# A third way of splitting the combined weights: 18 blocks of products in stage 3, R's sums bank by bank, S2's sum on VectorE, a scaled identity on ScalarE

## The chip, the cores and the metric

The kernel runs on one core of a Trainium2 chip. The metric is the device time of one execution in microseconds; the kernel before took 480.68 us (median of 3 runs, 479.33 to 481.21). A core has TensorE for matrix products (PE, its weight loads are listed as PEld), VectorE (DVE), ScalarE (ACT), GpSimd (POOL) and SyncE (SP), which here issues the transfers. SBUF is the on-chip memory, PSUM the banks that TensorE writes its products into.

## The reference

128 samples x of 64 channels and 1024 positions pass four convolutions of three taps, whose weights are scaled per sample by a style vector and normalised; the second doubles the length, the fourth halves it again. The input is added at the end.

```python
s = style @ mw.T + mb
weight = SCALE * w * s[:, None, :, None]
demod = lax.rsqrt(jnp.sum(weight * weight, axis=(2, 3)) + EPS)
weight = weight * demod[:, :, None, None]
# 'same':       conv of 3 taps, + b
# 'upsample':   transposed conv of stride 2, + b, then a blur of (1, 3, 3, 1) / 8 times 2
# 'downsample': a blur of (1, 3, 3, 1) / 8, then a conv of stride 2, + b
for i, typ in enumerate(('same', 'upsample', 'same', 'downsample')):
    out = _layer(out, style, weights[i], biases[i], mod_w[i], mod_b[i], typ)
return x + out
```

Nothing nonlinear stands between the layers, so for one sample they are one convolution of nine taps and stride one over x, with edge effects at the two ends.

## The kernel before

For each group of four samples (q, 32 of them) the kernel first multiplies the four layers' small weight matrices into one table of nine taps, and then runs this one convolution over the samples. All is in 32-bit floats. Four samples fill the 128 partitions twice (two of 64 channels in each), so a product stands as four matrix instructions, one for each quadrant of 64 x 64; the profile records each of them twice.

*The weights of a group* come in stages, each a set of small products in PSUM and copies that scale them per sample on ScalarE. `scale3` scales the last layer's weights (wd). `stage1_a` and `stage1_b` multiply them with the third layer's into S (five tap matrices; some are formed as sums and differences, which saves products). `share`, `share_copy` and `stage2_rest` multiply S with E, the second layer's taps with its blur, into R (seven matrices; two sums of pairs are kept beside them, formed by `r_sums` on GpSimd). `stage3_b` and `stage3_a` multiply R with the first layer's weights into the nine taps W. Products that are shared are made in `stage3_b`, in a bank of psA that is free just then; ScalarE copies them into psW, and `stage3_a` accumulates the rest on top.

*Combining.* The nine taps are used in groups of three positions (three kinds: a, b, c), and the convolution uses the Toom scheme: five products m0 to m4 with three taps each instead of nine. `combine_a` and `combine_b` on VectorE form the weights h1, h2, h3 from a, b, c; `residual` adds the identity matrix (the final "x +"), scaled per sample by a table t3, to the middle tap.

*The convolution.* `conv0` to `conv4` are these five products, 12 matrix instructions of 340 columns each. conv3, conv1, conv2 and conv0 accumulate one after the other in the same bank psA, and what stands there in between is picked up: `copy_m3` (ScalarE), `sum1` and `sum2` (VectorE). `sum2` runs after conv2: it writes 3 x m3 + psA into the bank Y, on which conv4 then accumulates, and subtracts psA from y1w. `outputs` scales the three result planes on ScalarE, and SyncE stores them.

*Order.* The program's order is written out by hand (`turn_of(q)` for q = 4 to 28, `early_turn` for the first four, a tail for the last three); each engine executes its own instructions strictly in that order and waits where data or a buffer is missing. A turn q works on four groups at a time: convolutions of q and n = q + 1, stage 2 and 3 of c = q + 2, stage 1 of s = q + 4. In a turn from q = 5 on TensorE runs: stage 2 of c, conv2 of q, `stage3_b` of c, conv4 of q, `stage3_a` of c, conv3 of n, `stage1_a` of s, conv0 of q, `stage1_b`, `share`, conv1 of n. psW, psS and psR share the same two PSUM banks (pool `ps_w`, one buffer), so each must be read out before the next is written. The lines of the profile are those of helpers: L753 is `product` (all five convolutions), L571 `same_row` (stage 3), L467 `chain_matmul` (stage 2), L389 `tap_matmul` (stage 1), L360 `scaled_copy` (ScalarE's scaled copies), L662 `sum_of` (VectorE), L588 `r_sums`, L445 and L442 the ends of `stage1_b`, L659 `residual`, L812 the subtraction in `sum2`, L726 and L731 `in1` and `in2` on GpSimd, L711 `in3` on VectorE.

## Time and profile before

| | |
|---|---|
| time of the kernel, median of 3 runs | 480.68 us (479.33, 480.68, 481.21) |
| profiled execution: span from first to last instruction | 478.0 us |
| granted clock of TensorE, mean | 0.997 |
| busy: TensorE, VectorE, ScalarE, GpSimd | 469.6, 417.5, 310.1, 163.5 us |
| convolutions of 340 columns (L753), three groups of it | 187.3, 63.9, 62.8 us |
| transfers | 70.70 MB, mean 148 GB/s |

Of the profiled execution the profile gives the span alone; the three times above are of executions without a profile, and the median lies 2.7 us above the span. In rows of groups the columns are the line, the engine, the operation, output and inputs, shapes and count, then busy time and mean duration of one in ns, and after the second bar the engine's idle time before them with what ended it. In rows of a timeline they are start and duration in us; several alike are merged, and in square brackets stands idle time ahead. Matrix instructions overlap, so that the start of the next is a better measure of a product's cost than its recorded duration.

### The profile page before, as it was taken

What the parts mean: (1) busy time and instruction counts of PE and PEld (TensorE: products, weight loads), DVE (VectorE), ACT (ScalarE), POOL (GpSimd) and SP (SyncE); (2) the same over time, 40 slices, a digit from 0 to 9 for tenths busy, and PEclk for the clock granted to TensorE, in tenths of its full rate; (3) what the DMA queues carried; (4) which work ended last, traced back from release to release, by engine and by line L of the source; (5) the groups of instructions that cost most, each with busy time, mean ns of one, the idle gap of its engine ahead of it and who ended that gap; (6) DMA issues with size and microseconds to landing.
All of it is one profiled execution on the core that took longest, in us unless ns stands there. A gap on an engine that the chain in (4) does not pass through costs nothing.

```text
span 478.0 us, 26721 instructions
## 1 busy us (share of the span) xinstructions
PE 469.6 (98%) x11928; PEld 346.4 (72%) x11928; DVE 417.5 (87%) x690; ACT 310.1 (65%) x708; POOL 163.5 (34%) x197
## 2 busy tenths in 40 slices
PE   8999999999999999999999999999999999999995
PEld 7877788777878876677776677766887777766652
DVE  5889998879889998899979899979989999999895
ACT  5565666667666676666667666667666768766352
POOL 3434032663335342243432233422434432333200
PEclk9999999999999999999999999999999999999998
DMA  5406365544445554345543455533455554445125
GB/s 175 158 28 200 114 195 192 150 139 144 139 150 157 173 173 127 122 151 160 171 149 120 131 170 152 173 127 126 145 169 162 162 154 146 152 146 170 61 91 191
DMA packets 50514, 70.70 MB, mean 148 GB/s; under 512 B 5664, under 2 KB 47328, under 8 KB 50400
## 3 DMA queue, kind: packets, MB, share of 16 engines
q1 hardware_dynamic: 49808, 68.32, 45.8%
q8 instruction: 93, 1.52, 1.5%
q10 hardware_dynamic: 592, 0.69, 0.5%
q14 instruction: 21, 0.17, 0.1%
HBM read 35.36 MB, written 33.62 MB: 144 GB/s over the span
## 4 chain that ended last, share of the span: by engine, by line
PE 95%; DVE 4%; issue 0%; ACT 0%; ACTq 0%; DVEq 0%
PE psA L753 45%; PE Y L753 11%; PE psR L467 9%; PE psA L571 7%; PE psW L571 7%; PE psS L389 6%; PE psR L533 4%; PE psA L467 2%; PE Y L994 2%; DVE H L662 1%; PE Y L180 1%; PE Y L336 1%; DVE G L662 0%; PE psM L204 0%; DVE o L832 0%
## 5 line engine op out<-in xcount | busy, mean ns | idle before, releaser
L753 PE MATMUL psA<-T,H 64*64 64x340 f32 x2304 | 187.3, 447 | 0.8 <-DVE y L662 0.7
L753 PEld LDWEIGHTS psA<-T,H 64*64 64x64 f32 x2304 | 89.9, 133 | 50.0 <-issue 3.1
L662 DVE SCALAR_TENSOR_TENSOR G<-X 128x1376 f32<-128x1376 f32 (+2 forms) x65 | 78.1, 1207 | 1.1 <-DMA X<-in_x 0.9
L726 POOL TENSOR_TENSOR T<-G 128x684 f32<-128x684 f32 x28 | 46.5, 1659 | 73.1 <-DVE G L662 73.1
L445 POOL TENSOR_TENSOR S<-S 128x128 f32<-128x128 f32 x28 | 22.1, 790 | 144.1 <-ACT S L360 136.8
L360 ACT ACTIVATE R<-psR,tC 128x448 f32<-128x448 f32 x63 | 36.5, 630 | 46.3 <-PE psR L467 26.7
L753 PE MATMUL psA<-T,Wf 64*64 64x340 f32 x768 | 63.9, 446 | 0.0
L753 PE MATMUL Y<-T,Wf 64*64 64x340 f32 x768 | 62.8, 451 | 0.1
L662 DVE SCALAR_TENSOR_TENSOR Y<-m,psA 128x340 f32<-128x340 f32 x64 | 33.1, 517 | 28.0 <-PE psA L753 26.6
L360 ACT ACTIVATE psW<-psA 128x128 f32<-128x128 f32 x100 | 19.3, 269 | 50.3 <-PE psA L571 46.2
L740 DVE TENSOR_TENSOR T<-G 128x1368 f32<-128x1368 f32 (+1 forms) x33 | 50.7, 1540 | 0.0
L360 ACT ACTIVATE Wf<-psW,t 128x256 f32<-128x256 f32 (+2 forms) x76 | 32.7, 479 | 26.5 <-PE psW L571 26.2
L711 DVE TENSOR_TENSOR T<-X 128x684 f32<-128x684 f32 x32 | 47.9, 1496 | 0.0
L467 PE MATMUL psR<-S,E 64*64 64x64 f32 (+1 forms) x1472 | 46.5, 238 | 0.0
L731 POOL TENSOR_TENSOR T<-G 128x684 f32<-128x684 f32 x28 | 46.5, 1660 | 0.0
L389 PEld LDWEIGHTS psS<-wd,w2n 64*64 64x64 f32 x1120 | 35.0, 133 | 13.3 <-ACT S L360 0.8
L467 PEld LDWEIGHTS psR<-S,E 64*64 64x64 f32 x1472 | 39.6, 134 | 5.2 <-ACT psR L490 0.2
L753 PEld LDWEIGHTS Y<-T,Wf 64*64 64x64 f32 x768 | 29.6, 132 | 18.0 <-DVE Y L662 0.7
L830 ACT ACTIVATE o<-psA,tb,td 128x340 f32<-128x340 f32 x63 | 37.0, 647 | 6.3 <-PE psA L753 6.3
L753 PEld LDWEIGHTS psA<-T,Wf 64*64 64x64 f32 x768 | 29.1, 133 | 15.1
L830 ACT ACTIVATE o<-Y,tb,td 128x340 f32<-128x340 f32 x63 | 36.6, 637 | 4.5 <-PE Y L753 2.7
L830 ACT ACTIVATE o<-y,tb,td 128x340 f32<-128x340 f32 x62 | 38.5, 679 | 0.6 <-DVE y L812 0.6
(165 smaller groups left out, 832.4 us busy)
## 6 DMA issues: line engine op xcount, KB each, us to landing
out<-o SPq DMA_DIRECT2D x167, 170.0 KB, 2.6
X<-in_x SPq DMA_DIRECT2D x150, 172.0 KB, 3.6
X<-in_x SPq DMA_DIRECT2D x14, 516.0 KB, 5.3
out<-o SPq DMA_DIRECT2D x6, 510.0 KB, 5.4
out<-o SPq DMA_DIRECT2D x2, 340.0 KB, 3.0
Xe<-in_x_ends SPq DMA_DIRECT2D x1, 512.0 KB, 6.7
out<-o ACTq DMA_DIRECT2D x3, 170.0 KB, 2.3
par<-in_params SPq DMA_DIRECT2D x2, 192.0 KB, 3.4
```

The costliest lines, as they stand in the source:

```text
L360: nc_a.activation(dst, src, AF.Copy, scale=f)
L389: nc.tensor.matmul(ps[r][cols, at * C : (at + n) * C], weight[rows], wd[c if r == 0 else 1 - c][rows, taps], start=first, stop=last, skip_ ...
L445: nc_g.tensor_add(t[:, :, 2], t[:, :, 2], t[:, :, 0])
L467: nc.tensor.matmul(dst[r][cols], weight[rows], st[c if r == 0 else 1 - c][rows, slots, :], start=False, stop=last, skip_group_check=True,)
L571: nc.tensor.matmul(dst[r][cols], weight[rows], t[rows, c, slots, :], start=first, stop=last, skip_group_check=True,)
L662: nc_v.scalar_tensor_tensor(out, x, f, y, op0=ALU.mult, op1=op)
L711: nc_v.tensor_sub(t[:, pairs, 0, :NJ], plane(X, 3, pairs), plane(X, 1, pairs))
L726: eng.tensor_add(t[:, :, 0, :NJ], plane(g, 2), plane(g, 1))
L731: eng.tensor_sub(t[:, :, 1, :NJ], plane(g, 2), plane(g, 1))
L740: nc_v.tensor_sub(t[:, pairs, :, :NJ], both(a, PL), both(b, 1))
L753: nc.tensor.matmul(ps[s][cols, :NB], w, Ts[q, tag][rows, c, i, g : g + NB], start=(g == 0 and m == 3), stop=(g == K - 1), skip_group_check ...
L830: nc_a.activation(dst, src, AF.Identity, bias=add, scale=d3)
```

## The change

Stage 3 is split anew. Before, two shared sums of pairs of R and 10 further blocks of 64 columns were made in `stage3_b`, 7 blocks in `stage3_a`. Now R has three sums of pairs (slots 7 to 9), one operation for each of its two banks; `stage3_b` multiplies them and makes 3 further blocks, and `stage3_a` makes 12 blocks: 18 in all for 19. ScalarE's copies into psW become two (each block written to two places) instead of four. The nine taps now lie in their natural order in W (`tap`, `TAPS`), and `stage3_a`'s result is scaled by kind with three tables t0, t0b, t0c, in six copies for two; `stage3_b`'s own result is two taps for five.

S is stored in another order (slots) and with other signs: even matrices at 2, 4, 6 and odd at 3, 5, with the sign in En (negated taps of E) instead of w2n and tBn. `stage1_b` forms on VectorE three matrices for two in one operation, and GpSimd's addition to S (L445) goes. `sum2` writes both banks of Y in one operation. `identity(n)`, two scaled copies on ScalarE after stage 2, makes x3, and `residual` adds it in one operation for two. In turns from q = 5 on the first third of conv0 of q moves ahead of `stage1_a`. The direct form of stage 1 (first groups) takes one product of three blocks for each tap.

```diff
...
@@ -293,12 +293,13 @@
     def table_B(bs):
         table(nc_g, tB, bs, ALT, DOWN, sc[:, 2, bs], sc[:, 1, bs])
 
-    def table_Bn(bs):
-        qs = slice(bs.start // 4, bs.stop // 4)
-        nc_g.tensor_scalar_mul(tBn[:, qs], tB[:, qs], -1.0)
-
     def table_0(bs):
         table(nc_g, t0, bs, ALT, ODD, sc[:, 0, bs], 1.0)
+
+
+    def table_0_kinds():
+        for t, f in ((t0b, 1.0 / 3.0), (t0c, -2.0)):
+            nc_g.tensor_scalar_mul(t, t0, f)
 
 
     def table_C(bs, eng=nc_g):
@@ -363,13 +364,17 @@
 
 
     w3x = const.tile([P, 5, C], F32, name="w3x")
-    w2n = const.tile([P, 5, C], F32, name="w2n")
+    w2n = const.tile([P, 2, C], F32, name="w2n")
+    En = const.tile([P, 4, C], F32, name="En")
 
     def split_weights():
         nc_g.tensor_copy(w3x[:, :K], w3)
-        nc_g.tensor_scalar_mul(w2n[:, :K], woi[2], -1.0)
-        for t, src in ((w3x, w3), (w2n, woi[2])):
-            nc_g.tensor_add(t[:, K:], src[:, : K - 1], src[:, 1:])
+        nc_g.tensor_add(w3x[:, K:], w3[:, : K - 1], w3[:, 1:])
+        nc_g.tensor_add(w2n, woi[2][:, : K - 1], woi[2][:, 1:])
+        nc_g.tensor_scalar_mul(w2n, w2n, -1.0)
+
+    def negated_taps():
+        nc_g.tensor_scalar_mul(En, E[:, 1:8:2], -1.0)
 
     DIRECT = 3
 
...
@@ -423,26 +429,26 @@
 
         ps = ps or unit(ps_w, f"psS{q}")
         wd = chain[q]
-        tap_matmul(ps, wd, 2, 2, w2n[:, 0, :], EVEN, first=True)
-        tap_matmul(ps, wd, 3, 2, w2n[:, 2, :], EVEN)
-        tap_matmul(ps, wd, 1, 1, w2n[:, 1, :], slice(1, 2))
+        tap_matmul(ps, wd, 3, 2, woi[2][:, 0, :], EVEN, first=True)
+        tap_matmul(ps, wd, 4, 2, woi[2][:, 2, :], EVEN)
+        tap_matmul(ps, wd, 2, 1, woi[2][:, 1, :], slice(1, 2))
         st, t = s_tiles(q)
         for r in range(2):
-            scaled_copy(nc_a, flat(st[r][:, :4]), ps[r][:, C : 5 * C], tBn[:, q, r : r + 1])
+            src = ps[r][:, 2 * C : 6 * C].rearrange("c (a o) -> c a o", o=C)
+            scaled_copy(nc_a, st[r][:, 0:7:2], src, tB[:, q, r : r + 1])
         chain[q] = wd, ps, st, t
 
     def stage1_b(q):
 
         wd, ps, st, t = chain[q]
-        tap_matmul(ps, wd, 2, 1, w2n[:, 3, :], slice(3, 4))
-        tap_matmul(ps, wd, 4, 1, w2n[:, 4, :], slice(4, 5), last=True)
+        tap_matmul(ps, wd, 3, 1, w2n[:, 0, :], slice(3, 4))
+        tap_matmul(ps, wd, 5, 1, w2n[:, 1, :], slice(4, 5), last=True)
         for r in range(2):
-            p1 = st[r][:, 0:1, :].to_broadcast([P, 2, C])
-            sums = ps[r][:, 2 * C : 6 * C].rearrange("c (a b o) -> c a b o", a=2, b=2)[:, :, 0]
+            p1 = st[r][:, 0:1, :].to_broadcast([P, K, C])
+            sums = ps[r][:, 3 * C : 6 * C].rearrange("c (a o) -> c a o", o=C)
             nc_v.scalar_tensor_tensor(
-                st[r][:, 4:6, :], sums, tB[:, q, r : r + 1], p1, op0=ALU.mult, op1=ALU.subtract
+                st[r][:, 3:6, :], sums, tB[:, q, r : r + 1], p1, op0=ALU.mult, op1=ALU.add
             )
-        nc_g.tensor_add(t[:, :, 2], t[:, :, 2], t[:, :, 0])
         chain[q] = st
         whole[q] = t
 
...
@@ -540,17 +547,17 @@
                     )
         if between:
             between()
-        t = r_pool.tile([P, 2, 9, C], F32, tag="R", name=f"R{q}")
+        t = r_pool.tile([P, 2, 10, C], F32, tag="R", name=f"R{q}")
         for r in range(2):
-            scaled_copy(engs[r], flat(t[:, r, :7]), ps[r][:, : 7 * C], tC[:, q, r : r + 1])
+            scaled_copy(engs[r], flat(t[:, r, :7]), ps[r][:, C : 8 * C], tC[:, q, r : r + 1])
         chain[q] = t
         return ps
 
 
-    TAPS = slice(3, 9, 2), slice(4, 9, 2), slice(0, 3)
+    TAPS = slice(0, 9, 3), slice(1, 9, 3), slice(2, 9, 3)
 
     def tap(kind, g):
-        return range(9)[TAPS[kind]][g]
+        return K * g + kind
 
     def new_w(q):
         Wq[q] = (
...
@@ -577,15 +584,20 @@
                     skip_group_check=True,
                 )
 
-    def stage3_out(q, ps, at, n, engs=(nc_a, nc_a)):
-        W = Wq[q][0]
+    def w_by_group(q, r):
+        return Wq[q][0][:, :, r].rearrange("c (g k) o -> c g k o", k=K)
+
+    def stage3_out(q, ps, kinds, engs=(nc_a, nc_a)):
         for r in range(2):
-            src = ps[r][:, : n * C].rearrange("c (a o) -> c a o", o=C)
-            scaled_copy(engs[r], W[:, at : at + n, r], src, t0[:, q, r : r + 1])
+            n = len(kinds)
+            src = ps[r][:, : n * K * C].rearrange("c (g k o) -> c g k o", k=n, o=C)
+            dst = w_by_group(q, r)[:, :, kinds[0] : kinds[0] + n]
+            scaled_copy(engs[r], dst, src, t0[:, q, r : r + 1])
 
     def r_sums(q, eng):
         t = chain[q]
-        eng.tensor_add(t[:, :, 7:9], t[:, :, 2:6:3], t[:, :, 3:7:3])
+        for r in range(2):
+            eng.tensor_add(t[:, r, 7:10], t[:, r, 0:6:2], t[:, r, 1:7:2])
 
     shared_w = {}
 
@@ -594,35 +606,36 @@
         new_w(q)
         t = chain[q]
         plan = (
-            (slice(0, 3), w0s[2][:, 2, :], slice(0, 7, 3)),
-            (slice(0, 2), w0s[2][:, 1, :], slice(1, 5, 3)),
-            (slice(0, 2), w0s[2][:, 0, :], slice(2, 6, 3)),
-            (slice(3, 4), w0s[0][:, 0, :], slice(0, 1)),
-            (slice(4, 5), w0s[1][:, 0, :], slice(1, 2)),
-            (slice(4, 5), w0s[1][:, 1, :], slice(0, 1)),
-            (slice(5, 7), w0s[0][:, 1, :], slice(7, 9)),
+            (slice(3, 4), w0s[1][:, 2, :], slice(5, 6)),
+            (slice(3, 4), w0s[1][:, 1, :], slice(6, 7)),
+            (slice(4, 5), w0s[2][:, 2, :], slice(6, 7)),
+            (slice(0, 3), woi[0][:, 1, :], slice(7, 10)),
         )
         for i, (at, weight, slots) in enumerate(plan):
             same_row(blocks(ps, at), weight, t, slots, i == 0, i == len(plan) - 1)
         pw = shared_w[q] = unit(ps_w, f"psW{q}")
-        src = blocks(ps, slice(5, 7))
-        for i, f in enumerate((1.0, 1.0 / 3.0)):
-            for dst, v in zip(blocks(pw, slice(i, i + 3, 2)), src):
-                scaled_copy(nc_a, dst, v, f)
-        stage3_out(q, ps, 0, 5)
+        for r in range(2):
+            src = ps[r][:, : K * C].rearrange("c (a o) -> c a o", o=C)
+            dst = pw[r][:, C : 7 * C].rearrange("c (a b o) -> c a b o", b=2, o=C)
+            nc_a.copy(dst, src[:, :, None, :].to_broadcast([P, K, 2, C]))
+        for r, src in enumerate(blocks(ps, slice(3, 5))):
+            scaled_copy(nc_a, Wq[q][0][:, 7:9, r], src, t0[:, q, r : r + 1])
 
     def stage3_a(q):
 
         t, pw = chain[q], shared_w.pop(q)
         plan = (
-            (slice(0, 3, 2), Wd[:, 0], slice(3, 7, 3)),
-            (slice(0, 3, 2), w0s[0][:, 2, :], slice(1, 5, 3)),
-            (slice(1, 4, 2), Wd[:, 1], slice(2, 6, 3)),
-            (slice(1, 2), w0s[1][:, 0, :], slice(4, 5)),
+            (slice(1, 6, 2), Wd[:, 0], slice(1, 6, 2)),
+            (slice(2, 7, 2), Wd[:, 1], slice(0, 5, 2)),
+            (slice(0, 7, 2), woi[0][:, 0, :], slice(0, 7, 2)),
+            (slice(3, 6, 2), woi[0][:, 2, :], slice(1, 4, 2)),
         )
         for i, (at, weight, slots) in enumerate(plan):
             same_row(blocks(pw, at), weight, t, slots, last=i == len(plan) - 1)
-        stage3_out(q, pw, 5, 4)
+        for kind, scale in enumerate((t0, t0b, t0c)):
+            at = slice(kind, 7, K)
+            for r, src in enumerate(blocks(pw, at)):
+                scaled_copy(nc_a, Wq[q][0][:, at, r], src, scale[:, q, r : r + 1])
 
     def stage3(q, part, pool=None, engs=(nc_a, nc_a)):
 
@@ -648,15 +661,17 @@
                     n == 1,
                     n == K * len(kinds),
                 )
-        stage3_out(q, ps, *((3, 6), (0, 3))[part], engs)
+        stage3_out(q, ps, kinds, engs)
         return ps
 
+    def identity(q):
+        for r in range(2):
+            nc_a.activation(x3[:, r], idn3, AF.Copy, scale=t3[:, q, r : r + 1])
+
     def residual(q):
 
-        W = Wq[q][0]
-        for r in range(2):
-            v = W[:, tap(1, 1), r, :]
-            nc_v.scalar_tensor_tensor(v, idn3, t3[:, q, r : r + 1], v, op0=ALU.mult, op1=ALU.add)
+        v = Wq[q][0][:, tap(1, 1)]
+        nc_v.tensor_add(v, v, x3)
 
     def sum_of(out, x, f, y, op=ALU.add):
         nc_v.scalar_tensor_tensor(out, x, f, y, op0=ALU.mult, op1=op)
@@ -806,8 +821,8 @@
     def sum2(q, steps=(0, 1)):
         if 0 in steps:
             m3 = m3c.pop(q)
-            for s, a in enumerate(banks(q)):
-                sum_of(Y[:, s, :NB], m3[:, s], 3.0, a[:, :NB])
+            for s, a in parts(q):
+                sum_of(Y[:, s, :NB], m3[:, s], 3.0, a)
         for s, a in parts(q) if 1 in steps else ():
             nc_v.tensor_sub(y1w[q][:, s], y1w[q][:, s], a)
 
...
@@ -1415,6 +1433,7 @@
         n, c, s = q + 1, q + 2, q + 4
         entry = q == FIRST
         stage2(c)
+        identity(n)
         if entry:
             sum2(q)
             conv4(q)
@@ -1440,6 +1459,8 @@
         if entry:
             copy_m3(n)
         outputs(q, 2)
+        if not entry:
+            conv0(q, 0)
         if s < NQ:
             stage1_a(s)
         if not entry:
@@ -1452,7 +1473,7 @@
         if q in SMALL:
             l, bs = SMALL[q]
             nc_v.memset(high(bs.stop - bs.start), 0.0)
-        conv0(q, *((2,) if entry else range(K)))
+        conv0(q, *((2,) if entry else (1, 2)))
         if entry:
             conv1(n, 0, 1)
         outputs(q, 1)
...
```

Three places of the program show the order. On TensorE, in the turn in which conv2 and conv4 work on group 14, from conv2 to conv3 (R is that of group 16; w0s, par and wsq hold forms of the first layer's weights); before:

```order
L753 MATMUL psA_4136<-T_14_4048,H_3868 64x340 x12
L571 MATMUL psA_4409<-R_4383,w0s_154 64x192 x4
L571 MATMUL psA_4409<-R_4383,w0s_154 64x128 x8
L571 MATMUL psA_4409<-R_4383,par 64x64 x4
L571 MATMUL psA_4409<-R_4383,w0s_153 64x64 x8
L571 MATMUL psA_4409<-R_4383,par 64x128 x4
L753 MATMUL Y<-T_14_4248,Wf_3867 64x340 x12
```

and now, to the end of stage 3:

```order
L768 MATMUL psA_4001<-T_14_3911,H_3743 64x340 x12
L578 MATMUL psA_4264<-R_4236,w0s_155 64x64 x8
L578 MATMUL psA_4264<-R_4236,w0s_156 64x64 x4
L578 MATMUL psA_4264<-R_4236,par 64x192 x4
L768 MATMUL Y<-T_14_4106,Wf_3742 64x340 x12
L578 MATMUL psW_0_4283<-R_4236,wsq 64x3x64 x2
L578 MATMUL psW_1_4284<-R_4236,wsq 64x3x64 x2
```

Between conv2 (into psA, with H) and conv4 (into Y) stood seven products with 12 blocks of 64 columns, and now stand four with 6; the products of R's sums (64x192) are the last of them. Behind conv4 the products into psW grow to three blocks each.

On ScalarE, the part of the same turn from the copies of R to the copies of S; before:

```order
L360 ACTIVATE R_4383<-psR_0_4295,tC 128x448
L360 ACTIVATE R_4383<-psR_1_4296,tC 128x448
L360 ACTIVATE psW_0_4440<-psA_4409 128x2x64
L360 ACTIVATE psW_1_4441<-psA_4409 128x2x64
L360 ACTIVATE psW_0_4440<-psA_4409 128x2x64
L360 ACTIVATE psW_1_4441<-psA_4409 128x2x64
L360 ACTIVATE Wf_4410<-psA_4409,t_137 128x5x64 x2
L360 ACTIVATE Wf_4410<-psW_0_4440,t_137 128x4x64
L360 ACTIVATE Wf_4410<-psW_1_4441,t_137 128x4x64
L830 ACTIVATE o_4497<-Y,tb,td 128x340 x2
L360 ACTIVATE S_4516<-psS_0_4502,tBn 128x256
```

and now:

```order
L361 ACTIVATE R_4236<-psR_1_4149,tC 128x448
L669 ACTIVATE x_158<-idn_157,t_139 128x64 x2
L620 COPY psW_0_4283<-psA_4264 128x384
L620 COPY psW_1_4284<-psA_4264 128x384
L361 ACTIVATE Wf_4265<-psA_4264,t_136 128x2x64 x2
L361 ACTIVATE Wf_4265<-psW_0_4283,t_136 128x3x64
L361 ACTIVATE Wf_4265<-psW_1_4284,t_136 128x3x64
L361 ACTIVATE Wf_4265<-psW_0_4283,t0b 128x2x64
L361 ACTIVATE Wf_4265<-psW_1_4284,t0b 128x2x64
L361 ACTIVATE Wf_4265<-psW_0_4283,t0c 128x2x64
L361 ACTIVATE Wf_4265<-psW_1_4284,t0c 128x2x64
L845 ACTIVATE o_4341<-Y,tb,td 128x340 x2
```

The two copies out of psW, ahead of the outputs from Y and the copies of S, have become six; the identity stands ahead of psW's copies.

On GpSimd, whose list in a turn is short; before:

```order
L726 TENSOR_TENSOR T_15_4321<-G_4251 128x2x342
L588 TENSOR_TENSOR R_4383<-R_4383 128x2x128
L731 TENSOR_TENSOR T_15_4321<-G_4251 128x2x342
L445 TENSOR_TENSOR S_4516<-S_4516 128x2x64
L726 TENSOR_TENSOR T_16_4604<-G_4524 128x2x342
```

and now:

```order
L741 TENSOR_TENSOR T_15_4174<-G_4109 128x2x342
L600 TENSOR_TENSOR R_4236<-R_4236 128x192 x2
L746 TENSOR_TENSOR T_15_4174<-G_4109 128x2x342
L741 TENSOR_TENSOR T_16_4447<-G_4372 128x2x342
L600 TENSOR_TENSOR R_4509<-R_4509 128x192 x2
```

The sum of R is two operations, one for a bank, and the operation on S is gone.

77 lines of the change are left out of this document (42 added, 35 removed).

## The prediction, made before the result was known

> **What bounds the kernel now.** I read the engines' shares and the chain of waits first, on the page of the kernel before.
>
> ```profile
> PE 469.6 (98%) x11928; PEld 346.4 (72%) x11928; DVE 417.5 (87%) x690; ACT 310.1 (65%) x708; POOL 163.5 (34%) x197
> PE 95%; DVE 4%; issue 0%; ACT 0%; ACTq 0%; DVEq 0%
> ```
>
> TensorE is busy for 98% of the span and 95% of the chain that ended last is its own. So time is lost or won where TensorE has fewer or more columns to stream, or where it stands still. Next comes the length of one steady turn (q = 5 to 28; busy time by stretches, each from one start of stage 2 to the next):
>
> ```profile
> 203.05:216.89 13.84, 13.84 (x392) 9.79 (x388) 12.68 (x20) 9.78 (x24) 4.80 (x4) 1.00 0.50 156
> 216.89:230.73 13.84, 13.84 (x392) 9.79 (x388) 12.72 (x21) 9.64 (x24) 4.84 (x4) 1.00 0.51 157
> ```
>
> A turn is 13.84 us, at a granted clock of 1.00, and VectorE has 1.1 us to spare in it, ScalarE 4. Then the timeline of one turn, TensorE first (start, duration, operation):
>
> ```profile
> 218.64 1.90 PE L753 MATMUL psA<-T,H 64*64 64x340 f32 x24
> 220.36 0.94 PE L571 MATMUL psA<-R,w0s 64*64 64x192 f32 x24
> 221.12 0.29 PE L571 MATMUL psA<-R,par 64*64 64x64 f32 x8
> 221.24 0.41 PE L571 MATMUL psA<-R,w0s 64*64 64x64 f32 x16
> 221.47 0.40 PE L571 MATMUL psA<-R,par 64*64 64x128 f32 x8
> 221.73 1.95 PE L753 MATMUL Y<-T,Wf 64*64 64x340 f32 x24
> 223.49 0.40 PE L571 MATMUL psW<-R,wsq 64*64 64x128 f32 x8
> 223.71 0.40 PE L571 MATMUL psW<-R,par 64*64 64x128 f32 x8
> ...
> 224.26 1.90 PE L753 MATMUL psA<-T,H 64*64 64x340 f32 x24
> 225.98 0.73 PE L389 MATMUL psS<-wd,w2n 64*64 64x128 f32 x24
> 226.53 1.90 PE L753 MATMUL psA<-T,Wf 64*64 64x340 f32 x24
> 228.25 0.41 PE L389 MATMUL psS<-wd,w2n 64*64 64x64 f32 x16
> ...
> 228.83 1.90 PE L753 MATMUL psA<-T,H 64*64 64x340 f32 x24
> 230.55 0.40 PE L467 MATMUL psR<-S,E 64*64 64x128 f32 x8
> ```
>
> The order is conv2 (218.64), stage3_b (220.36 to 221.73, into psA), conv4 (into Y, 221.73), stage3_a (223.49, into psW), conv3 (224.26), stage1_a (225.98), conv0, stage1_b, conv1. Eight records are one product of the table with its four quadrants. Starts give the price of one: 64 columns 0.115 (221.24 to 221.47 is two), 128 columns 0.22 (223.49 to 223.71), hence 192 columns 0.32 (220.36 to 221.12 is one of 192 and two of 128), and by the same slope 256 columns 0.43. The last look is at VectorE beside it:
>
> ```profile
> 217.81 1.85 DVE L711 TENSOR_TENSOR T<-X 128x684 f32<-128x684 f32 x1
> 220.61 1.07 DVE L662 SCALAR_TENSOR_TENSOR Y<-m,psA 128x340 f32<-128x340 f32 x2 [0.95 <-PE psA L753]
> 221.59 0.85 DVE L812 TENSOR_TENSOR y<-y,psA 128x680 f32<-128x680 f32 x1
> 222.36 0.56 DVE L662 SCALAR_TENSOR_TENSOR H<-Wf 128x384 f32<-128x384 f32 x1
> 222.84 0.47 DVE L659 SCALAR_TENSOR_TENSOR Wf<-idn,t,Wf 128x64 f32<-128x64 f32 x2
> 223.35 0.56 DVE L662 SCALAR_TENSOR_TENSOR H<-H,Wf 128x384 f32<-128x384 f32 x1
> ```
>
> This decides. VectorE waits 0.95 us for conv2, starts the sums into Y at 220.61 (0.25 after stage3_b's start), ends at 221.68, and conv4, which accumulates onto Y, starts 0.05 later. So already now the work that TensorE has between conv2 and conv4, stage3_b with 1.33 us by the prices above (0.32 + 0.44 + 0.115 + 0.23 + 0.22), is just as long as the wait for Y (1.37).
>
> **The change part by part.** *Products.* stage3_b falls from 12 blocks of 64 columns in 7 products to 6 in 4 (three of 64, one of 192), stage3_a grows from 7 blocks in 4 products to 12 in 4 (192, 192, 256, 128). Stage 1 and stage 2 keep their blocks (7 and 20). In columns alone a turn loses one block: stage3_b 1.33 becomes 0.345 + 0.32 = 0.665, stage3_a 0.77 (223.49 to 224.26) becomes 2 x 0.32 + 0.43 + 0.22 = 1.29, together 0.14 less.
>
> *The wait for Y.* But Y still cannot be ready before conv2 has ended and VectorE has summed. The price of the merged sum comes from these groups:
>
> ```profile
> L662 DVE SCALAR_TENSOR_TENSOR Y<-m,psA 128x340 f32<-128x340 f32 x64 | 33.1, 517 | 28.0 <-PE psA L753 26.6
> L662 DVE SCALAR_TENSOR_TENSOR y<-psA,m 128x680 f32<-128x680 f32 x32 | 27.6, 862 | 7.4 <-PE psA L753 5.9 <-PE psW L571 1.3
> ```
>
> One operation of 680 columns with an operand in PSUM takes 862 ns; I take 0.86 for the merged sum (not less than 0.68, twice the slope of 0.345 per 340 columns without its fixed part; not more than the 1.07 of the two). The 28.0 us of idle time over 32 tiles show that nearly every turn has this wait. conv4 then starts 0.25 + 0.86 + 0.05 = 1.16 after stage3_b's start instead of 1.37, a gain of 0.21. TensorE is through with stage3_b after 0.665 and stands still for 0.5. What is left of the products, stage3_a, is 1.29 instead of 0.77, a loss of 0.52. A turn becomes 0.31 longer: the five blocks that moved behind conv4 were the cover of the sum, and their new place has no wait to cover. With the bounds of the sum, 0.13 to 0.52. VectorE has nothing late in conv3: h3, which conv3 waits for, ended 3.30 after the sum's start (223.91 for 220.61) and now ends at most 3.1 after it, with the 0.21 saved; conv3 starts 1.16 + 1.76 + 1.29 - 0.25 = 3.96 after it.
>
> *GpSimd's sums of R.* The single sum of 256 columns becomes two of 192.
>
> ```profile
> 217.25 1.68 POOL L726 TENSOR_TENSOR T<-G 128x684 f32<-128x684 f32 x1 [2.61 <-DVE G L662]
> 220.17 0.73 POOL L588 TENSOR_TENSOR R<-R 128x256 f32<-128x256 f32 x1 [1.25 <-ACT R L360]
> 218.94 1.16 ACT L360 ACTIVATE R<-psR,tC 128x448 f32<-128x448 f32 x2 [0.93 <-POOL T L726]
> ```
>
> 0.95 us for 428 more columns is 2.2 ns a column, so 192 take about 0.59. The first bank is copied at 219.57 and summed by 220.24, the second by about 220.80, 0.44 after stage3_b's start; the three products ahead of it are through after 0.345, so stage3_b ends near 0.44 + 0.05 + 0.32 = 0.81. That is inside the 1.16 of Y, which is the cover of this cost: 0.35 are left. Without the cover it would be 0.15 a turn.
>
> *An edge of GpSimd.* In the rows above VectorE's T<-X starts at 217.81 while GpSimd runs until 218.93 and takes 1.85, where VectorE's own sum of this size takes 0.87:
>
> ```profile
> L726 DVE TENSOR_TENSOR T<-G 128x684 f32<-128x684 f32 x4 | 3.5, 873 | 0.1
> ```
>  The page "SBUF — State Buffer" of the Trainium skill, section "SBUF: two separate sides", says that GpSimd and a VectorE operation with two SBUF inputs hold a shared port exclusively, the later one waiting for the whole of the other; by that rule, 218.93 + 0.73 = 219.66, and the trace agrees. It speaks against R's sums on GpSimd; its result is the third rival below.
>
> *ScalarE.* Behind conv3 two copies of 256 columns become six, two of 192 and four of 128; the copies of stage 3's psW become two of 384; two scaled identities come after R.
>
> ```profile
> 222.00 0.77 ACT L360 ACTIVATE psW<-psA 128x128 f32<-128x128 f32 x4 [1.90 <-PE psA L571]
> 224.54 0.84 ACT L360 ACTIVATE Wf<-psW,t 128x256 f32<-128x256 f32 x2 [0.93 <-PE psW L571]
> 225.27 1.16 ACT L830 ACTIVATE o<-Y,tb,td 128x340 f32<-128x340 f32 x2
> 226.75 0.84 ACT L360 ACTIVATE S<-psS,tBn 128x256 f32<-128x256 f32 x2 [0.32 <-PE psS L389]
> 228.08 1.25 ACT L830 ACTIVATE o<-y,tb,td 128x340 f32<-128x340 f32 x2
> 229.44 0.63 ACT L490 COPY psR<-psA 128x256 f32<-128x256 f32 x2
> ...
> L360 ACT ACTIVATE psW<-psA 128x128 f32<-128x128 f32 x100 | 19.3, 269 | 50.3 <-PE psA L571 46.2
> L360 ACT ACTIVATE Wf<-psW,t 128x256 f32<-128x256 f32 x50 | 21.0, 470 | 22.0 <-PE psW L571 22.0
> L360 ACT ACTIVATE Wf<-psW,t 128x192 f32<-128x192 f32 x13 | 4.8, 418 | 0.4 <-PE psW L571 0.3 <-PE Y L914 0.2
> ```
>
> The identities and psW's copies fall into the idle 1.90 and beside conv4. The six: 192 columns 418 ns; 128 with a scale per partition lie between 269 (fixed scale) and 418, I take 366 (as far below 418 as the 470 of 256 columns lies above). Two of 470 take 0.84, an overlap of 0.1; so 2 x 418 + 4 x 366, less five overlaps, is 1.80 instead of 0.84: 0.96 more. stage1_a reuses psW, but the change puts a third of conv0 (0.57 of 1.72) ahead of it, so it starts at 2.29 after conv3's start and the six are done at 0.28 + 1.80 = 2.08. stage1_a ends at 2.84, the copies of S start 0.22 later as now and end at 3.06 + 0.84 = 3.90, against a stage1_b at 2.84 + 1.15 = 3.99. psR's copies end 3.2 to 3.3 after S's start (226.75 to 230.07 here, where VectorE's side work held them up by 0.1), 6.2 to 6.3, against a stage 2 at 3.99 + 0.23 + 0.35 + 1.72 = 6.29. ScalarE's cover is used up there: I take 0.03 a turn, and 0.15 if the six copies take 418 each.
>
> *The rest* is small: S2's sum moves from GpSimd into VectorE's existing operation (192 columns for 128, 0.07 each, inside VectorE's 1.1 us), the signs move into tables made once, and the first turns save a few product starts, which I count at nothing.
>
> **The sum.** 24 turns x (0.31 + 0.03) = 8.1: the span of 478.0 becomes 486.1. The median of the runs shown, 480.68, lies 2.7 above this span, launch and end outside it, which stays: 488.8.
>
> **The rivals.** (1) *The count decides:* TensorE does one block less and conv4 is not held by Y. Then 0.14 x 24 = 3.4 us are won, 477.3, faster. It needs the sum of Y to be ready 0.67 after stage3_b's start, 0.42 after VectorE's start; one bank alone takes 0.517 now. Against it stands the 0.05 between the sum's end and conv4. (2) *ScalarE becomes the second wait:* the six copies at 418 or more delay stage1_b or stage 2 by 0.15 instead of 0.03: 488.8 + 2.9 = 491.7. For it: margins near nothing. Against: ScalarE is 65% busy and its order has idle time ahead of R. (3) *GpSimd's sums come last:* a VectorE sum with both inputs in SBUF holds them up by its own 0.73; then stage3_b ends at 0.44 + 0.73 + 0.05 + 0.32 = 1.54 instead of 1.16: 0.38 x 24 = 9.1 more, 497.9 if in each turn; if in half of them, 493.4. Against: VectorE's T<-X ends before the sums begin here, and VectorE then idles. (4) *A wash:* the merged sum at its low bound (0.13 a turn, 3.1 us) and something given back elsewhere, such as port time that GpSimd's dropped sum of S frees for VectorE: 481 to 483.
>
> **How the numbers follow.** The forecast has 0.62, its own range is 485.5 to 491. ScalarE's wait 0.13, GpSimd's 0.10, the wash 0.08, the count 0.07. The range of 483.5 to 494.0 leaves out the faster case, the wash and the worst of GpSimd's, under 2 in 10. Within 0.5% of 480.68, about what a measurement tells from no change, is 478.3 to 483.1. Faster 0.07, same 0.08, slower 0.85.
>
> **What would show it.** Right: conv2's last records followed by stage3_b in about 0.8 us, then TensorE idle or stretched until 0.05 after the single Y sum's end; 1.16 from stage3_b's start to conv4's and 3.05 from conv4's to conv3's; turns of about 14.2 us; TensorE's share of busy time lower. Wrong: conv4 starting before the sum's end in the records (rival 1), a TensorE gap before stage1_b or stage 2 that ScalarE ended (2), or one inside stage3_b that GpSimd ended (3) and that outlasts Y.

## The result and the profile after

The changed kernel takes 491.88 us (median of 4 runs, 490.82 to 492.56), the kernel before 480.0 us in the same comparison (4 runs, 479.02 to 481.21): 1.0245 times as long, with a 95% interval of 1.0223 to 1.0266. The prediction was 488.8 us in a range of 483.5 to 494.0. The profiled execution has a span of 489.5 us for 478.0, so 11.5 us are to be explained. Two of the changed kernel's four executions (490.82 and 491.31) had a mean granted clock of 0.998, the other two (492.46 and 492.56) one of 0.995 and 0.996.

From the page of the changed kernel, the engines' shares, the chain that ended last, and the groups of the sum into Y and of the sums of R; then two steady turns, by stretches from one start of stage 2 to the next:

```profile
PE 475.5 (97%) x11232; PEld 341.1 (70%) x11232; DVE 409.5 (84%) x627; ACT 341.0 (70%) x822; POOL 149.3 (30%) x194
...
PE 74%; DVE 5%; issue 1%; ACT 0%; ACTq 0%; DVEq 0%
...
L677 DVE SCALAR_TENSOR_TENSOR Y<-m,psA 128x680 f32<-128x680 f32 x32 | 27.9, 871 | 28.5 <-PE psA L768 28.4
...
L600 POOL TENSOR_TENSOR R<-R 128x192 f32<-128x192 f32 x48 | 28.4, 612 | 24.2 <-ACT R L361 24.2
```

```profile
208.84:223.06 14.22, 14.08 (x364) 10.00 (x362) 12.41 (x18) 10.91 (x28) 4.40 (x4) 1.00 0.50 152
223.06:237.28 14.22, 14.08 (x364) 9.83 (x362) 12.58 (x19) 10.92 (x28) 4.40 (x4) 1.00 0.50 152
```

TensorE has 696 instruction records fewer (11232 for 11928) and a longer span. The chain's shares add up to 80% here (before, 99%), so its 74% and 95% are not to be set against each other; the turns are. A turn is 14.22 us, where it was 13.84, at the same granted clock of 1.00. TensorE's busy time hides most of that: a product that waits for its operand is recorded as a longer one, and 14.08 of 14.22 count as busy. The timeline of the turn shows where the 0.38 lie (all engines by start; start, duration):

```profile
225.00 1.90 PE L768 MATMUL psA<-T,H 64*64 64x340 f32 x24
225.30 1.16 ACT L361 ACTIVATE R<-psR,tC 128x448 f32<-128x448 f32 x2 [0.39 <-PE psR L473]
226.01 1.14 POOL L600 TENSOR_TENSOR R<-R 128x192 f32<-128x192 f32 x2 [0.69 <-ACT R L361]
226.35 0.58 ACT L669 ACTIVATE x<-idn,t 128x64 f32<-128x64 f32 x2
...
226.72 0.53 PE L578 MATMUL psA<-R,w0s 64*64 64x64 f32 x24
226.96 0.87 DVE L677 SCALAR_TENSOR_TENSOR Y<-m,psA 128x680 f32<-128x680 f32 x1 [0.92 <-PE psA L768]
...
227.06 0.68 PE L578 MATMUL psA<-R,par 64*64 64x192 f32 x8
...
227.89 1.35 PEld L768 LDWEIGHTS Y<-T,Wf 64*64 64x64 f32 x24 [0.49 <-DVE Y L677]
227.89 1.95 PE L768 MATMUL Y<-T,Wf 64*64 64x340 f32 x24
...
229.66 0.83 PE L578 MATMUL psW<-R,wsq 64*64 64x192 f32 x16
...
230.96 1.90 PE L768 MATMUL psA<-T,H 64*64 64x340 f32 x24
...
231.23 0.73 ACT L361 ACTIVATE Wf<-psW,t 128x192 f32<-128x192 f32 x2 [1.98 <-PE psW L578]
...
232.35 0.64 ACT L361 ACTIVATE Wf<-psW,t0c 128x128 f32<-128x128 f32 x2
...
234.01 0.84 ACT L361 ACTIVATE S<-psS,tB 128x256 f32<-128x256 f32 x2
...
236.48 0.66 ACT L496 COPY psR<-psA 128x256 f32<-128x256 f32 x2
...
237.28 0.40 PE L473 MATMUL psR<-S,E 64*64 64x128 f32 x8
```

stage3_b starts at 226.72, VectorE's single sum into Y runs from 226.96 to 227.83, and conv4 starts at 227.89, 0.06 behind its end. TensorE's weight loads stand for 0.49 us until the sum is there. stage3_a, behind conv4, lasts from 229.66 to 230.96, 1.30 us. From stage3_b's start to conv4's it is 1.17, from conv4's to conv3's 3.07: the forecast was 1.16 and 3.05. Over the whole execution the waits list this stand 22 times (engine, its line, and what it waited for; us in all, times, longest):

```profile
PEld Y L768 <- DVE Y L677: 10.1, 22, 0.5
```

So a turn is much as forecast, and the missing 3 us lie elsewhere. TensorE's timeline gives the start of conv4 for each of the 32 groups (where one conv4 stands in several rows, the largest is taken). Between these starts the two profiled executions part as follows (us):

| stretch | before | after | difference |
|---|---|---|---|
| until the first conv4 | 31.29 | 31.43 | +0.1 |
| five intervals to the sixth conv4 (first turns and the entry, q = 4) | 75.96 | 80.25 | +4.3 |
| 24 intervals, the turns with the new stage 3 | 343.44 | 350.67 | +7.2 |
| the rest | 27.3 | 27.2 | -0.1 |

The five early intervals are 14.96, 14.50, 14.73, 15.41 and 16.36 before and 15.18, 14.61, 14.90, 18.09 and 17.47 after: 2.68 and 1.11 lie in the last two alone. In the waits of the changed kernel a new one belongs to this place:

```profile
DVE Wf L674 <- ACT x L669: 6.4, 5, 2.0
```

VectorE's `residual` waits for the scaled identity, five times, once in each group up to q = 4. The timeline of the changed kernel at the fourth of them and behind it:

```profile
76.36 1.16 ACT L361 ACTIVATE R<-psR,tC 128x448 f32<-128x448 f32 x2 [0.99 <-PE psR L540]
77.41 0.58 ACT L669 ACTIVATE x<-idn,t 128x64 f32<-128x64 f32 x2
...
78.02 0.29 DVE L674 TENSOR_TENSOR Wf<-Wf,x 128x128 f32<-128x128 f32 x1 [1.95 <-ACT x L669]
...
87.12 1.68 POOL L741 TENSOR_TENSOR T<-G 128x684 f32<-128x684 f32 x1 [12.07 <-DVE G L677]
87.35 0.17 DVE L942 TENSOR_TENSOR oc<-Y,dm 128x16 f32<-128x16 f32 x1
87.56 1.28 DVE L943 TENSOR_SCALAR oc<-oc,par_s 128x16 f32<-128x16 f32 x1
...
88.75 0.85 DVE L677 SCALAR_TENSOR_TENSOR y<-psA,m 128x680 f32<-128x680 f32 x1
...
89.75 0.80 PE L768 MATMUL psA<-T,H 64*64 64x340 f32 x8 [2.51 <-DVE y L677]
```

In a steady turn stage 2 runs ahead of conv2, so that ScalarE is through with R and the identity (226.93 above) before VectorE has even begun its sum into Y. In the early turns stage 2 runs behind conv2, beside that sum. ScalarE has the copies of R in front of the identity (76.36), and these wait for stage 2; VectorE comes to `residual` first and loses 1.95 us. Its operations follow without a gap from there to its sum y at 88.75, and there a second delay comes on top: an operation of 16 columns (L943) lasts 1.28 us, from 87.56 until GpSimd's sum T<-G ends at 88.80. The next convolution waits 2.51 us for y. In the kernel before, the same place reads:

```profile
85.26 0.23 DVE L927 TENSOR_SCALAR oc<-oc,par_s 128x16 f32<-128x16 f32 x1
...
86.93 0.46 POOL L445 TENSOR_TENSOR S<-S 128x128 f32<-128x128 f32 x1 [11.73 <-ACT S L360]
...
87.35 1.65 POOL L726 TENSOR_TENSOR T<-G 128x684 f32<-128x684 f32 x1
```

There GpSimd's sum of S (L445) stood ahead of T<-G and waited for ScalarE until 86.93, long after VectorE's small operation at 85.26, which took 0.23. The change removes that sum, so that T<-G starts with G and meets the small operation.

### The profile page after: what moved, and what is told of

It reads as the page before. It is cut to its first block, busy times and chain, and to the rows that moved or that the text cites. A ratio compares the mean times of both kernels' runs of the same rounds, so it can differ in the third digit from the quotient of the medians.

```text
span 489.5 us, 25400 instructions
## 1 busy us (share of the span) xinstructions
PE 475.5 (97%) x11232; PEld 341.1 (70%) x11232; DVE 409.5 (84%) x627; ACT 341.0 (70%) x822; POOL 149.3 (30%) x194
## 4 chain that ended last, share of the span: by engine, by line
PE 74%; DVE 5%; issue 1%; ACT 0%; ACTq 0%; DVEq 0%
PE psA L768 38%; PE Y L768 10%; PE psR L473 9%; PE psW L578 7%; PE psS L394 4%; DVE Y L677 3%; PE psA L473 2%; PE Y L1010 2%; PE psA L578 1%; PE psR L540 1%; DVE o L847 0%; DVE T L755 0%; PE psE L1010 0%; ACT o L845 0%; DVE Oe L1124 0%
## 5 line engine op out<-in xcount | busy, mean ns | idle before, releaser
L768 PE MATMUL psA<-T,Wf 64*64 64x340 f32 x768 | 68.4, 446 | 0.0
L361 ACT ACTIVATE Wf<-psW,t 128x192 f32<-128x192 f32 (+1 forms) x76 | 30.1, 445 | 51.2 <-PE psW L578 51.0
L677 DVE SCALAR_TENSOR_TENSOR Y<-m,psA 128x680 f32<-128x680 f32 x32 | 27.9, 871 | 28.5 <-PE psA L768 28.4
L768 PEld LDWEIGHTS Y<-T,Wf 64*64 64x64 f32 x768 | 28.6, 132 | 26.3 <-DVE Y L677 10.1
L620 ACT COPY psW<-psA 128x384 f32<-128x384 f32 x50 | 21.2, 467 | 26.8 <-PE psA L578 23.1
L677 DVE SCALAR_TENSOR_TENSOR H<-Wf 128x384 f32<-128x384 f32 x64 | 39.1, 611 | 0.0
L677 DVE SCALAR_TENSOR_TENSOR H<-H,Wf 128x384 f32<-128x384 f32 x64 | 35.7, 559 | 2.2
L600 POOL TENSOR_TENSOR R<-R 128x192 f32<-128x192 f32 x48 | 28.4, 612 | 24.2 <-ACT R L361 24.2
L449 DVE SCALAR_TENSOR_TENSOR S<-psS,tB,S 128x192 f32<-128x192 f32 x56 | 20.7, 412 | 17.2 <-ACT m L807 14.8
```

The lines of the kernel that those rows point to most:

```text
L361: nc_a.activation(dst, src, AF.Copy, scale=f)
L600: eng.tensor_add(t[:, r, 7:10], t[:, r, 0:6:2], t[:, r, 1:7:2])
L620: nc_a.copy(dst, src[:, :, None, :].to_broadcast([P, K, 2, C]))
L677: nc_v.scalar_tensor_tensor(out, x, f, y, op0=ALU.mult, op1=op)
L768: nc.tensor.matmul(ps[s][cols, :NB], w, Ts[q, tag][rows, c, i, g : g + NB], start=(g == 0 and m == 3), stop=(g == K - 1), skip_group_check ...
```

## The experiments

The theory at this point: in the steady turns TensorE waits for Y because stage 3's moved blocks were its cover; in the early turns VectorE waits for the identity. Its rivals were the prediction's (ScalarE's six copies, GpSimd's sums of R), and that the 18 blocks are sound and only lack another cover. Times are medians; each ratio is to the kernel before, run on the same chip beside it (480.0 to 480.35 us), with its 95% interval. "Turn" is an undisturbed steady turn of the profile. "Early" is the sum of the five early intervals of the profiled execution (75.96 before, 80.25 after). The 81.31 and the 81.87 hold about 1.7 us of a lower granted clock, which the last section shows, and are not to be set against 80.25 as they stand.

| kernel | us | ratio | turn | early |
|---|---|---|---|---|
| before | 480.1 | 1 | 13.84 | 75.96 |
| after | 491.88 | 1.0245 (1.0223 to 1.0266) | 14.22 | 80.25 |
| after, identity first | 487.14 | 1.0163 (1.0127 to 1.0200) | 14.22 | 76.50 |
| after, share as cover | 515.78 | 1.0752 (1.0728 to 1.0775) | 15.33 | |
| both of these | 511.51 | 1.0671 (1.0635 to 1.0708) | 15.33 | |
| after, old stage 3 | 481.58 | 1.0028 (1.0011 to 1.0046) | 13.79 | 81.31 |
| after, Y summed in two | 497.10 | 1.0352 (1.0321 to 1.0383) | 14.41 | 80.43 |
| before, Y summed in one | 476.69 | 0.9937 (0.9916 to 0.9958) | 13.75 | 75.84 |
| after, R summed in one | 492.54 | 1.0252 (1.0225 to 1.0279) | 14.24 | 81.87 |
| old stage 3, identity first | 477.91 | 0.9950 (0.9926 to 0.9974) | 13.80 | 76.86 |
| the same, conv0 undivided | 476.96 | 0.9927 (0.9901 to 0.9952) | 13.75 | 76.85 |
| after, identity first, conv0 undivided | 495.22 | 1.0314 (1.0296 to 1.0333) | 14.57 | |
| the best | 475.20 | 0.9910 (0.9886 to 0.9933) | 13.75 | 76.03 |

### Identity ahead of stage 2

The two scaled copies move ahead of stage 2's copies on ScalarE, in the turns up to q = 4 alone.

```diff
 # early_turn
+        identity(n)
         stage2(c)
-        identity(n)
 # turn_of
+        if entry:
+            identity(n)
         stage2(c)
-        identity(n)
+        if not entry:
+            identity(n)
```

> The changed kernel with the scaled identity ahead of stage 2 in ScalarE's order in the first four turns and in turn 4; the steady turns are untouched. If the identity behind stage 2's copies holds VectorE up there (five waits of 6.4 us together) and this makes the 4.6 us by which the steady turns begin late: 487 to 488.5, the first stage3_b about 3 us earlier. Rival, in which the late start comes from GpSimd, whose sum T now starts earlier and blocks a small VectorE operation (2.5 us of one wait of TensorE): 2 us or more of it stay, 490 to 491.

487.14 us: 4.7 less than the changed kernel. The steady turn stays at 14.22, and the early intervals fall from 80.25 to 76.50. The timeline of this kernel at the place shown above (VectorE and TensorE):

```profile
75.42 0.28 DVE L674 TENSOR_TENSOR Wf<-Wf,x 128x128 f32<-128x128 f32 x1
...
84.94 1.30 DVE L943 TENSOR_SCALAR oc<-oc,par_s 128x16 f32<-128x16 f32 x1
...
87.16 0.80 PE L768 MATMUL psA<-T,H 64*64 64x340 f32 x8 [0.61 <-DVE y L677]
```

`residual` follows without a wait, and TensorE's wait for y falls from 2.51 to 0.61 although the small operation still lasts 1.30. So the identity's place on ScalarE costs 3.7 us by the early intervals of the profiled executions and 4.7 by the medians, and the meeting with GpSimd about 0.6 on top.

### Another cover for Y

If only cover is missing between conv2 and conv4, `share` of the next group (0.35 us of products into psA) can stand there.

```diff
             conv2(q)
             r_sums(c, nc_g)
+            if sharing(q):
+                share_sums(c + 1)
             sum2(q)
 ...
             combine_a(n)
+            if sharing(q):
+                share(c + 1, banks(q))
             conv4(q)
 ...
-        if sharing(q):
-            share_sums(c + 1)
 ...
-            share(c + 1, banks(q))
             share_copy(c + 1)
```

> The changed kernel with the three products of S's sums (share) moved from behind stage1_b to between stage3_b and conv4, and VectorE's sum of S ahead of the sum into Y. Wait for Y (my theory): TensorE has 0.35 us more to do where it stands still for 0.5, so conv4 still starts 1.17 after stage3_b's start, a turn falls from 14.22 to about 13.87, and 23 turns win about 8 us: 484. Rival, in which conv4 is held by nothing but TensorE's own products: conv4 starts 0.35 later, 1.5 after stage3_b's start, the turn and the time stay at 14.22 and 492.

> The two edits together. If they act in different turns, their gains add up: 479.5 to 480.5, level with the kernel before. If GpSimd's collision is what delays the start: about 482.5. If the products only move: 488 or more.

515.78 us, and 511.51 with the identity first. Both theories missed: the turn is 15.33. The edit brought a wait of its own. The waits of this kernel, and its timeline in one turn (VectorE, then TensorE):

```profile
PEld psA L473 <- DVE y L827: 24.6, 23, 1.6
```

```profile
235.35 0.87 DVE L677 SCALAR_TENSOR_TENSOR Y<-m,psA 128x680 f32<-128x680 f32 x1 [0.65 <-PE psA L768]
236.13 0.85 DVE L827 TENSOR_TENSOR y<-y,psA 128x680 f32<-128x680 f32 x1
...
235.10 0.53 PE L578 MATMUL psA<-R,w0s 64*64 64x64 f32 x24
235.45 0.85 PE L578 MATMUL psA<-R,par 64*64 64x192 f32 x8
237.04 0.46 PE L473 MATMUL psA<-S,E 64*64 64x64 f32 x16 [0.74 <-DVE y L827]
...
237.44 1.90 PE L768 MATMUL Y<-T,Wf 64*64 64x340 f32 x24
```

`share` writes psA and is held until VectorE's second reading of psA, the subtraction from y, has ended (236.98; `share` starts at 237.04). conv4 stands behind it on the same engine, and starts 2.34 after stage3_b instead of 1.17. So the run shows that this cover is none; it doesn't show what a cover without that wait would bring. The difference of 4.3 between the two kernels repeats the price of the identity.

### The old stage 3 in the changed kernel

Stage 3 goes back to its 19 blocks (12 of them in `stage3_b`), with its tap order and two copies out of psW; all else is as in the change. The first of these kernels leaves a part of the result out; the instructions are the same. The two later kernels (identity first; then conv0 undivided behind `stage1_a` too) shift psW's blocks by one, as the new stage 2 moved R's blocks in psR by one, and compute all. So the place of psW's blocks is the cause; that one block is overwritten there instead of added to is inferred and not shown.

```diff
-            (slice(3, 4), w0s[1][:, 2, :], slice(5, 6)),
-            (slice(3, 4), w0s[1][:, 1, :], slice(6, 7)),
-            (slice(4, 5), w0s[2][:, 2, :], slice(6, 7)),
-            (slice(0, 3), woi[0][:, 1, :], slice(7, 10)),
+            (slice(0, 3), w0s[2][:, 2, :], slice(0, 7, 3)),
+            (slice(0, 2), w0s[2][:, 1, :], slice(1, 5, 3)),
+            (slice(0, 2), w0s[2][:, 0, :], slice(2, 6, 3)),
+            (slice(3, 4), w0s[0][:, 0, :], slice(0, 1)),
+            (slice(4, 5), w0s[1][:, 0, :], slice(1, 2)),
+            (slice(4, 5), w0s[1][:, 1, :], slice(0, 1)),
+            (slice(5, 7), w0s[0][:, 1, :], slice(7, 9)),
 ...
 # third kernel
-        if not entry:
-            conv0(q, 0)
 ...
-        conv0(q, *((2,) if entry else (1, 2)))
+        conv0(q, *((2,) if entry else range(K)))
```

> The changed kernel with stage 3 as before (19 blocks, 12 of them ahead of conv4, one sum of R of 256 columns, old order of the taps), all other edits kept. Wait for Y: stage3_b takes 1.33 again, stage3_a 0.77, a turn 13.8 to 13.85, 24 turns win 9 us: 483, and the rest of the loss (the first turns) stays. Rival, in which the other edits (identity, S's sum on VectorE, conv0's place) cost the steady turns: the turn stays above 14.0 and the time above 486.

> Stage 3 as before in the changed kernel (the 19 blocks; psW's four blocks lie one block further up) and the identity ahead of stage 2 in the first five turns. If the loss of the steady turns (stage 3) and of the first turns (identity) are separate: 481.6 - 4.7 = 476.9, 3 us faster than the kernel before, turns of 13.80. If they overlap: 479 to 481.

> The same with conv0 undivided behind stage1_a again. With two copies out of psW instead of six nothing waits there, and the copies of S come 0.57 earlier in ScalarE's order, so that conv1 takes 1.72 instead of 1.76 before stage 2: 13.76 a turn, 1 us less, 475.9. Rival, in which conv0's place is free either way: 476.9.

481.58, 477.91 and 476.96 us. The identity's place is worth 3.7 us here, for the 4.7 expected. A steady turn of the first kernel, by stretches, and the start of stage3_b, the sum into Y and conv4 in it (TensorE, then VectorE, then TensorE):

```profile
219.24:233.03 13.79, 13.79 (x388) 9.96 (x386) 12.72 (x19) 10.23 (x26) 4.02 (x3) 1.00 0.51 156
...
222.89 0.94 PE L578 MATMUL psA<-R,w0s 64*64 64x192 f32 x24
...
223.14 0.87 DVE L671 SCALAR_TENSOR_TENSOR Y<-m,psA 128x680 f32<-128x680 f32 x1 [0.90 <-PE psA L762]
...
224.22 1.90 PE L762 MATMUL Y<-T,Wf 64*64 64x340 f32 x24
```

The busy time is the whole turn again. 14.22 falls to 13.79: the new split of stage 3, with its sums and copies, costs 0.43 a turn, with one block less to multiply. Y is ready (224.01) before the old `stage3_b` ends, and conv4 starts 1.33 after `stage3_b`'s start, just the products' price. Undoing conv0's move takes another 0.05 (13.80 to 13.75).

### Y in one sum or in two

```diff
 # changed kernel: two sums; kernel before: the reverse
-            for s, a in parts(q):
-                sum_of(Y[:, s, :NB], m3[:, s], 3.0, a)
+            for s, a in enumerate(banks(q)):
+                sum_of(Y[:, s, :NB], m3[:, s], 3.0, a[:, :NB])
```

> The changed kernel with the sum into Y as two operations again, one for a bank (1.07 us for 0.87). Wait for Y: conv4 starts 1.37 after stage3_b's start instead of 1.17, a turn is 14.42, 24 turns lose 4.9 us: 496.8. Rival, in which TensorE's own products set conv4's start: 491.9 as the changed kernel.

> The kernel before with the sum into Y as one operation of both banks, nothing else. Y would then be ready 1.17 after stage3_b's start, and TensorE's 12 blocks there take 1.33: conv4 starts 1.33 after it instead of 1.37, 0.04 a turn, 1 us: 479.3, not to be told from no change by the time, but by the starts. If the Y sum were what the turn is bound by: 0.2 a turn, 475.5.

The changed kernel with two sums takes 497.10 us, 14.41 a turn. Its timeline (VectorE's row is from the same turn):

```profile
227.51 0.53 PE L578 MATMUL psA<-R,w0s 64*64 64x64 f32 x24
...
228.88 1.95 PE L768 MATMUL Y<-T,Wf 64*64 64x340 f32 x24 [0.33 <-DVE Y L677]
...
227.76 1.07 DVE L677 SCALAR_TENSOR_TENSOR Y<-m,psA 128x340 f32<-128x340 f32 x2 [0.91 <-PE psA L768]
```

conv4 starts 1.37 after stage3_b, 0.05 behind the end of the longer sums: the time goes up with the sum, 0.19 a turn for 0.20 of the sum. With the new stage 3 it is VectorE's sum that sets conv4's start, not the number of products.

The kernel before with one sum takes 476.69 us, less than the 479.3 expected and nearer to the rival's 475.5; but its turn falls by 0.09, not by the rival's 0.2 and not by 0.04 either: conv4 starts 1.33 after stage3_b instead of 1.37, and the next step follows 1.72 after conv4 instead of 1.77, which is also conv4's length with the old stage 3 and with R summed in one, where it does not wait for Y either. 24 x 0.09 is 2.2 of the 3.4 us. In the profiled executions the 24 intervals fall by 2.8 together (the one that took 16.29 takes 15.65), for a reason that no run here shows, and where the last 0.6 of the medians lies is open.

### R summed in one operation

```diff
-        for r in range(2):
-            eng.tensor_add(t[:, r, 7:10], t[:, r, 0:6:2], t[:, r, 1:7:2])
+        eng.tensor_add(t[:, :, 7:10], t[:, :, 0:6:2], t[:, :, 1:7:2])
```

> The changed kernel with GpSimd's sums of R as one operation of 384 columns instead of one of 192 for each bank. By the price of 2.2 ns a column it takes 1.0 us and ends 0.82 after stage3_b's start, 0.27 later than the two; the products behind it end 1.2 after that start, as late as Y. If Y is what conv4 waits for: a turn loses 0.05 at most, 492 to 493.5. Rival, in which R's sums hold conv4 up: 0.27 a turn, 498.

492.54 us, 14.24 a turn. The timeline (TensorE, then GpSimd):

```profile
227.68 0.53 PE L578 MATMUL psA<-R,w0s 64*64 64x64 f32 x24
228.55 0.56 PE L578 MATMUL psA<-R,par 64*64 64x192 f32 x8 [0.34 <-POOL R L599]
228.92 1.90 PE L767 MATMUL Y<-T,Wf 64*64 64x340 f32 x24
...
227.50 1.00 POOL L599 TENSOR_TENSOR R<-R 128x384 f32<-128x384 f32 x1 [1.21 <-ACT R L361]
```

The sum ends at 228.50, 0.82 after stage3_b's start instead of 0.43 (227.15 for 226.72), and the last product waits for it. That is 0.39 later, not the 0.27 of the expectation. conv4 starts at 1.24 instead of 1.17, but it no longer waits for Y and takes 1.72 instead of 1.77, so the turn is only 0.02 longer. So GpSimd's sums had 0.32 us of room under Y's sum (0.35 forecast), and bank by bank is worth next to nothing here.

### conv0 undivided in the changed kernel

The edit is that of the third kernel with the old stage 3, with the identity first.

> The changed kernel with the identity ahead of stage 2 (487.1) and conv0 undivided behind stage1_a. If the six copies out of psW are covered only by conv0's first third: they end 2.03 after conv3's start, stage1_a would start at 1.72 and waits about 0.35; 0.04 come back before stage 2; 0.3 a turn, 7 us: 494. Rival, in which the six copies cost TensorE nothing wherever conv0 stands: 486 to 487.

495.22 us, 14.57 a turn against 14.22. The waits of this kernel:

```profile
PEld psS L394 <- ACT Wf L361: 12.7, 24, 0.6
```

`stage1_a` waits for the six copies out of psW, 0.53 us in each of 24 turns, since both use the same banks. The third of conv0 ahead of it is what covers the copies, and the 0.05 that it costs is well spent where there are six; with the two copies of the old stage 3 it only costs.

### The best of it

The third kernel with the old stage 3, and in turn 3 VectorE's small operations ahead of the last part of G, so that they are over when GpSimd starts T<-G.

```diff
+        if twice:
+            extra(q, 1)
         if q > 1:
             in_g2(c)
 ...
-        extra(q, 1)
+        if not twice:
+            extra(q, 1)
```

> Stage 3 as before, identity ahead, conv0 undivided (476.96), and in turn 3 VectorE's small operations on the constants ahead of G's last part instead of behind it, so that GpSimd's sum T cannot start before them. If GpSimd's running T is what makes the operation of 16 columns take 1.3 us: it takes 0.23 again and TensorE's wait in conv0 there shrinks from 1.40 to 0.7: 0.7 us less, 476.3. Rival, in which the operation waits for something else: 477.

475.20 us, 0.9910 of the kernel before (0.9886 to 0.9933), the fastest here, though its interval meets those of the kernels at 476.69, 476.96 and 477.91. The small operation and GpSimd's sum in its timeline (VectorE, then GpSimd):

```profile
83.56 0.24 DVE L937 TENSOR_SCALAR oc<-oc,par_s 128x16 f32<-128x16 f32 x1
...
84.71 1.66 POOL L735 TENSOR_TENSOR T<-G 128x684 f32<-128x684 f32 x1 [11.05 <-DVE G L671]
```

0.24 us again. The interval in which it lies falls from 16.07 to 15.24, by 0.83 for the 0.7 expected; the median falls by 1.8, and what the rest is no run here shows. What remains of the change in this kernel is, in the main, the single sum of Y, the sum of S2 on VectorE and the scaled identity.

## Why the prediction was right, and where it was off

*Products and the wait for Y: right.* 1.17 from stage3_b to conv4 for 1.16, stage3_a 1.30 for 1.29, the sum into Y 0.87 for 0.86, a stand of 0.49 for 0.5. Both halves were tested apart. The old stage 3 in the changed kernel takes 0.43 off a turn, and a second operation for Y adds 0.19. So the 0.38 are made up, to 0.01, of 0.43 for the new split of stage 3 with the single sum in place, -0.09 that the single sum gives the old stage 3, and 0.05 for conv0's move. Forecast were 0.31 for the first two (measured 0.34) and 0.03 for ScalarE.

*GpSimd's sums of R: right.* 612 ns each in the mean (0.59 forecast), hidden under Y with the room that was worked out; one operation of 1.00 us costs 0.02 a turn.

*ScalarE: right in the sizes, wrong in the place of the 0.03.* The six copies end 2.03 after conv3's start (232.99 for 230.96; 2.08 forecast), S's copies 3.89 (3.90), psR's 6.18 (6.2 to 6.3), with stage 2 at 6.32 (6.29). But the old stage 3, with two copies, has the same loss: it goes only when conv0 is undivided again. It is conv0's third ahead of `stage1_a`, which makes S's copies and all behind them later, and not the six copies, that uses up ScalarE's cover. The six copies would be a wait of their own (0.35 a turn) without that third.

*The rest: the step that failed.* The first turns were counted "at nothing", and of the identities it was said that they "fall into the idle 1.90 and beside conv4". That holds in the steady turns. In the five early groups stage 2 stands beside VectorE's sum, ScalarE's idle time lies ahead of R's copies, and the identity comes behind them, too late for `residual`: most of the 4.3 us of the early intervals, of which the run with the identity first gives back 3.75 in the profile and 4.7 by medians. The lower clock of the last section, in two of the changed kernel's four executions, would fit the difference; those two left no profile, so it is not shown. 4.3 + 7.2 is the 11.5 of the span.

*What was luck.* The 24 turns cost 7.2 in the profiled executions, for 8.1 forecast. By the measured 0.38 they would cost 9.1; but turns that were longer than 13.84 before for other reasons (15.13, 16.29 and 14.36 for q = 5, 10 and 20) take 14.34, 16.23 and 14.21 now, which was not foreseen. And 491.88 lies outside the 485.5 to 491 that the prediction gave its own mechanism. It lies inside the wider range because that had room for ScalarE and GpSimd in the steady turns, and the first turns used it up.

*The rivals.* The count decided nothing: one block less made the turn longer. GpSimd's sums did not come last. The wash did not come either: the merged sum took 0.87 and not its low bound, and GpSimd's dropped sum of S gave no time back but let T<-G meet a small operation. 491.7 us, the price of ScalarE as a second wait, is near the measured time, but not for its reason: S's and psR's copies cost 0.05 a turn, and what ScalarE cost beyond the forecast was in the first five turns.

*Slips in the working.* Twice 0.345 is 0.69 and not 0.68, and psR's copies end by their own terms at 6.26 to 6.36 and not at 6.2 to 6.3; neither changes the forecast. The 0.73 by which T<-X ends behind GpSimd, in the part on an edge of GpSimd and in the third rival, stands in no row as the time of such a sum; it is the distance from GpSimd's end to the very end that it is said to explain. Alone such a sum takes 0.87, which would have ended at 219.80, 0.14 after the end in the trace, so that agreement is rougher than it reads. And the 2.7 us between the median and the span are not all outside the span: the changed kernel's profiled execution took 491.31 us for a span of 489.5, 1.8 more, and the rest is the distance of one execution from the median of several.

*Open* is whether 18 blocks pay with a cover that does not wait for VectorE. `share` could not be one in psA; no other was tried.

## What to carry to other kernels

Work between a producer and a wait is cover, and its price is not its columns: taking five blocks out of the place where TensorE waited anyway, and putting them where it does not wait, cost 0.43 us a turn while the count fell. Before work is moved to an engine with idle time, its place is to be looked up in every form of the loop, the first turns too: which instruction is ahead of it on the queue there, and how soon its result is used. And when an operation is removed from an engine off the path, what stood behind it starts earlier and may meet something: that was 0.6 to 0.8 us here.
